# Half expert tiles through the full tiles' products, and another order of steps at the end of the state space layer

## The chip, the cores and the metric

The kernel runs on one core of a Trainium2 chip. The metric is the device time of one execution in microseconds (us), lower is better. The time before is 1714.96 us, the median of three runs (1714.86 to 1715.92).

## What is computed

The input u is 2 x 2048 tokens of 256 features. Four layers follow each other, each with a layernorm ahead of it and a residual sum behind it:

```
x = u
x = x + state_space(layernorm(x))   # projection to z, x, B, C, dt; causal convolution of 4 taps and silu;
                                    # scan h = h*exp(dt*A) + dt*x*B, y = h.C + D*x; y*silu(z), RMS norm, projection
x = x + experts(layernorm(x))       # 8 experts, every token goes to its best 2
x = x + attention(layernorm(x))     # 16 heads, over the batch dimension (2 entries)
x = x + experts(layernorm(x))       # the same weights again

experts(x):
    scores = x @ Wr.T + br                       # softmax; the two best by scores + biases, weights made to sum to 1
    y[n] = (silu(x @ Wl1[n][:, :512] + bl1a) * (x @ Wl1[n][:, 512:] + bl1b)) @ Wl2[n] + bl2
    out = sum over a token's two experts of weight * y[n]
```

All data are float32. An expert's matrices have 256 x 1024 (1 MB) and 512 x 256 (0.5 MB) elements.

## The kernel before

**Experts.** Class `Experts` computes an expert layer as a list of tiles: 256 token slots (two halves of 128) of one expert each. A routing step (`prepare`) ranks the experts for a group of 512 tokens (there are eight groups, `order`), counts by two products with 128 x 32 outputs (`pk`, L363 and L364) how many tokens each expert has so far, and so gives each token its slot. `enter` then writes the tokens' numbers and weights into a table in DRAM, by eight indirect transfers a group, issued by POOL (L433); it is a generator that gives control back after each of them, in the second layer after every other one.

A tile is started when its slots are full. `plan_early` chooses full tiles while groups still come in ("early" tiles, named `fe` in the first layer and `ge` in the second); `plan` chooses the rest from the final counts (`f` and `g`). In the first layer 21 early tiles (fe0 to fe20) are planned behind groups 3 to 7, in the second 9. What an expert has beyond whole tiles of 256 may fit a half tile of 128 slots: `plan` makes five half tiles per layer (`NIN`), and two more that run only if a count says so (`tc.If(beyond > 0)`).

Per tile: `rows` loads the tile's part of the table (SP, L656), `load` the expert's matrices and biases (SP, L668 to L674), `gather` the tokens (POOL, L683). `turn` transposes them on TensorE (`pxs`, L709; copy `xT`, L713). `up` computes the two products with Wl1 and gates them: for a full tile four parts, `up_part`, of four products each, with the weights' 128 columns standing in the array and 256 tokens moving (L722), then silu on ACT (`sa`, L730) and bias and product on DVE (`gT`, L731). `down` computes the product with Wl2 (`pf`, L792), adds bias and weight (L804, L805), and adds the rows to the residual in DRAM by indirect transfers (L816).

A half tile takes another way in `up` and `fold`: the tokens stand and 512 columns of Wl1 move (L750), ACT and DVE copy the two results `u` of 128 x 512 to SBUF, and eight transposes (`put`, L773) turn them back; then come four silu steps (L778) and four gating steps (L779) of 128 x 128. The transposes are issued in `fold`, behind the `down` of the tile before.

**Order of the work.** SP runs in the written order throughout; inside `run` POOL, ACT and DVE do too. Elsewhere the framework's scheduler orders PE, ACT, DVE and POOL. The state space layer steps through 32 chunks of 128 tokens (`chunk_front`, `chunk_back`, `chunk_out`). Three lists of generators are stepped between its parts: `aside` (projection and routing of other groups), `late` (`entering`: the table transfers, and behind them `plan_early`; each is also placed on POOL behind the chunk's POOL instruction just before) and `tiles` (`ffn.early`: the early tiles, which use PSUM bank B alone, with two buffers). Behind the last chunk the kernel finishes `aside`, then `late`, then plans, then finishes the early tiles; then `run` works through the other tiles with three tiles of lookahead. The attention layer does the same with `last`, whose early tiles go between attention's steps; it calls `last.plan()` behind all of them.

Lines: routing L300 to L410, `enter` L412 to L450, `plan_early` L452 to L513, `plan` from L515, tiles L648 to L894, state space layer L899 to L1242, attention L1256 to L1508.

Of the kernel before, what the change touches and what calls it, by code (L numbers as in the profile page):

```python
# [46 lines left out]
def kernel(  # L47
# [35 lines left out]
    def bank(tag, name):  # L83
        return ps.tile([P, 512], F32, tag=tag, name=name)
# [195 lines left out]
    class Experts:  # L280
# [454 lines left out]
        def up(self, i, between=None):  # L735
            t = self.ts[i]
            nm = t["nm"]
            pool = fe if i % 2 else self.f2
            t["gT"] = pool.tile([P, NHT, TT], F32, tag="gT", name=f"gT_{nm}", bufs=1)
            if t["nh"] == 2:  # L740
                for j in range(NHT):
                    self.up_part(t, j, "AB"[j % 2])
                    if between is not None and j == 1:
                        between()
                return

            for q in range(2):
                p = bank("AB"[q], f"pab_{nm}_{q}")
                for k in range(KD):
                    nc.tensor.matmul(  # L750
                        p,
                        t["xT"][:, k, :],
                        t["w1"][:, k, q * FH : (q + 1) * FH],
                        start=(k == 0),
                        stop=(k == KD - 1),
                    )
                u = self.f2.tile([P, FH], F32, tag=f"u{q}", name=f"u{q}_{nm}", bufs=1)
                if q:
                    nc.vector.tensor_copy(u, p)
                else:  # L760
                    nc.scalar.copy(u, p)
                t["u", q] = u

        def fold(self, i):
            t = self.ts[i]
            nm = t["nm"]
            if t["nh"] == 2:
                return
            ps2 = []
            for q in range(2):  # L770
                p = bank("AB"[q], f"put_{nm}_{q}")
                for j in range(NHT):
                    nc.tensor.transpose(p[:, j * P : (j + 1) * P], t["u", q][:, j * P : (j + 1) * P], ident)  # L773
                ps2.append(p)
            sa = self.f2.tile([P, FH], F32, tag="sh", name=f"sh_{nm}", bufs=1)
            for j in range(NHT):
                c = slice(j * P, (j + 1) * P)
                nc.scalar.activation(sa[:, c], ps2[0][:, c], AF.Silu, bias=t["b1"][:, j : j + 1])  # L778
                nc.vector.scalar_tensor_tensor(  # L779
                    t["gT"][:, j, :P], ps2[1][:, c], t["b1"][:, NHT + j : NHT + j + 1], sa[:, c], ALU.add, ALU.mult  # L780
                )

        def down(self, i, tag, then):
            t = self.ts.pop(i)
# [67 lines left out]
        def run(self):  # L852
# [3 lines left out]
            with (  # L856
# [8 lines left out]
                for i in range(first, n - 1):  # L865
                    self.fetch(i + ahead + 2, i + ahead + 1, gather=False)
                    if i == first + 6:
                        with tc.manual_schedule(engines={mybir.EngineType.PE}):
                            beyond = nc.values_load(self.beyond[0:1, 0:1], min_val=0, max_val=NHF - NIN)
                            self.up(i)  # L870
                    else:
                        self.up(i)
                    self.turn(i + 1)
                    if i > first:
                        self.down(i - 1, "C", i + ahead)
                    else:
                        for h in range(2):
                            self.gather(i + ahead, h)
                    self.fold(i)
                    if i == first + 2:  # L880
                        yield
                self.up(n - 1, lambda: self.down(n - 2, "C", None))
                self.down(n - 1, "C", None)
                with tc.If(beyond > 0):
                    for tile in self.more:
                        i = len(self.seq)
                        self.seq.append(tile)
                        self.fetch(i + 1, i + 1)
                        self.turn(i)
                        self.up(i)  # L890
                        self.fold(i)
                        self.down(i, "C", None)

    ffn = Experts("f", tc.dram_tile([NT + TT, DM], F32, name="resid"))  # L894
# [3 lines left out]
    with tc.tile_pool(name="ssm1", bufs=1) as s1, tc.tile_pool(name="ssm2", bufs=2) as s2:  # L898
# [306 lines left out]

        def entering(n, group):
            if n < len(order):
                for _ in range(4 if n < 4 else 9):
                    yield
            yield from ffn.enter(*group)  # L1210
            if n in EARLY:
                ffn.plan_early(n, EARLY[n], group[2])
# [25 lines left out]
            done = (b, s, t, y)  # L1238
        chunk_out(*done)
        aside.add(routing(*done[:2]))  # L1240
        aside.rest()
        late.rest()  # L1242
    ssm_w.__exit__(None, None, None)

    attw = ctx.enter_context(tc.tile_pool(name="attw", bufs=1))
    w_qkv_sb = attw.tile([P, KD, 3, AW], F32, name="w_qkv_sb")
    w_o_sb = attw.tile([P, NA, DM], F32, name="w_o_sb")
    ffn.plan()
    tiles.rest()
    late = ffn.run()  # L1250
    next(late)
# [8 lines left out]
    with tc.tile_pool(name="att1", bufs=1) as a1, tc.tile_pool(name="att2", bufs=2) as a2:  # L1260
# [36 lines left out]
        def entered():  # L1297
            while routed:
                n, group = routed.pop(0)
                yield from last.enter(*group)  # L1300
                if n in EARLY:
                    last.plan_early(n, EARLY[n], group[2])
                    tiles.step()
# [200 lines left out]
        while aside.waiting:  # L1504
            aside.step()
            tiles.step()
        last.plan()
        tiles.rest()  # L1508

    for _ in last.run():  # L1510
# [62 lines left out]
```

## Time and profile before

| | |
|---|---|
| median of three runs | 1714.96 us |
| the profiled execution | 1728.29 us |
| its span, first to last instruction | 1726.6 us |
| mean granted TensorE clock | 0.97 |
| busy: PE / DVE / POOL / ACT | 1595.6 / 900.0 / 734.6 / 673.9 us |
| DMA | 231.27 MB, mean 134 GB/s |
| chain that ended last: PE / DVE / DMA / POOL | 66% / 11% / 10% / 5% |
| half tiles' products `pab_f`, `pab_g` (L750) | 40 + 40 instructions of 128 x 512, mean 592 ns |
| their transposes `put_f`, `put_g` (L773) | 40 + 40 of 128 x 128, mean 273 ns |
| table transfers `table_f` from 655 to 690 us | 15, median 958 ns on POOL |

All profile rows come from one profiled execution, which is slower than the median. Times in a timeline count from the span's start. "PE" is matrix products on TensorE (transposes too), "PEld" the loads of the standing operand, "SPq" SP's queue of transfers. The length of a product's row includes the time until its last result is out, so products that follow each other overlap in the timeline; the chain of waits shows them end to end. A name stands for all buffers of that name: `pab_fe` is the first layer's early tiles, `pab_f` the others.

### The profile page before, as it was taken

Reading aid. Unit: us, or ns where it says so; the run is one execution under the profiler, and the core shown is the slowest. Engines: PE = TensorE matmul, PEld = TensorE weight load, DVE = VectorE, ACT = ScalarE, POOL = GpSimd, SP = SyncE. Lnnn points to the kernel's source line nnn. Section 1 sums busy time; section 2 is a strip of 40 time slices with the busy share of each in tenths; the row PEclk is TensorE's granted clock in tenths of the full one; section 3 lists DMA queues with packets and bytes.
Section 4 is the critical chain, followed back from the end, with each engine's and each line's share of the span. In section 5 each row is a group of like instructions: output and inputs, shape, how many; then the busy total and the mean of one; then the engine's idle time right before and its main releaser. Section 6 shows DMA issues by size and latency. Waiting matters only on the chain.

```text
span 1726.6 us, 21824 instructions
## 1 busy us (share of the span) xinstructions
PE 1595.6 (92%) x6928; PEld 1182.0 (68%) x6928; DVE 900.0 (52%) x2481; ACT 673.9 (39%) x1348; POOL 734.6 (43%) x702
## 2 busy tenths in 40 slices
PE   6997888989989996999998999899999799999997
PEld 4565555766767775788884475465768678888886
DVE  6877888838557465222237648457454522222222
ACT  4886877856556542223332102001120222333322
POOL 3346456446446565444442003403241643545443
PEclk9998998999989998999999999999999999999998
DMA  4121211734435353789842413606453668888882
GB/s 154 50 73 27 86 62 32 229 99 144 112 70 173 86 169 84 205 246 322 229 112 77 85 39 63 86 14 135 141 117 103 143 185 242 227 223 224 229 213 45
DMA packets 174742, 231.27 MB, mean 134 GB/s; under 512 B 45920, under 2 KB 138080, under 8 KB 174368
## 3 DMA queue, kind: packets, MB, share of 16 engines
q1 hardware_dynamic: 143520, 193.42, 37.7%
q0 software_dynamic: 31104, 36.42, 11.8%
q8 instruction: 56, 0.92, 0.2%
q14 instruction: 62, 0.51, 0.1%
HBM read 192.72 MB, written 37.06 MB: 133 GB/s over the span
## 4 chain that ended last, share of the span: by engine, by line
PE 66%; DVE 11%; DMA 10%; POOL 5%; issue 3%; ACT 3%; SPq 1%; DVEq 0%; POOLq 0%; ACTq 0%
PE pab_g L722 8%; PE pao L1462 6%; PE pq L1368 5%; PE pab_fe L722 5%; PE pab_f L722 4%; PE pf_g L792 4%; PE pab_ge L722 3%; PE pvd L1442 3%; PE pf_fe L792 3%; DVE xc L1047 3%; PE pk L1368 3%; PE pf_f L792 2%; PE pi L1143 2%; DMA lb<-sums 2%; DMA out_dram<-y_g,tab_g 2%
## 5 line engine op out<-in xcount | busy, mean ns | idle before, releaser
L722 PE MATMUL pab_fe<-xT_fe,w_fe 128*128 128x256 f32 x672 | 160.8, 395 | 26.9 <-DVE gT_fe L731 19.7
L722 PEld LDWEIGHTS pab_fe<-xT_fe,w_fe 128*128 128x128 f32 x672 | 130.7, 198 | 55.2 <-DVE gT_fe L731 24.3
L722 PE MATMUL pab_g<-xT_g,w_g 128*128 128x256 f32 x736 | 162.9, 379 | 0.0
L722 PEld LDWEIGHTS pab_g<-xT_g,w_g 128*128 128x128 f32 x736 | 139.4, 190 | 19.1 <-ACT xT_g L713 0.4
L816 POOL DMA_INDIRECT out_dram<-y_g,tab_g x51 | 80.3, 1574 | 141.4 <-DVE y_g L805 67.1
L1368 PE MATMUL pq<-w_qkv_sb,axT 128*128 128x512 f32 x256 | 117.9, 600 | 0.4 <-DVE qk L1387 0.4
L1047 DVE SCALAR_TENSOR_TENSOR xc<-pre,conv_w_sb,xc 128x512 f32<-128x512 f32 x144 | 112.4, 790 | 5.9 <-ACT xc L1039 5.2
L1462 PE MATMUL pao<-w_o_sb,o 128*128 128x256 f32 x512 | 112.4, 380 | 1.2 <-DVE o L1450 1.2
L1462 PEld LDWEIGHTS pao<-w_o_sb,o 128*128 128x128 f32 x512 | 96.9, 190 | 17.5 <-DVE o L1450 2.4
L731 DVE SCALAR_TENSOR_TENSOR gT_g<-pab_g,b_g,sa_g 128x256 f32<-128x256 f32 x92 | 44.5, 484 | 117.5 <-ACT sa_g L730 103.9
L730 ACT ACTIVATE sa_g<-pab_g,b_g 128x256 f32<-128x256 f32 x92 | 43.5, 473 | 154.4 <-PE pab_g L722 135.8
L433 POOL DMA_INDIRECT table_g<-pay_g,at_g x64 | 62.4, 975 | 88.0 <-DVE w_g L409 55.0
L1030 PE MATMUL pc<-xT,w_in_sb 128*128 128x512 f32 x192 | 94.8, 623 | 0.4 <-ACT xc L1039 0.4
L792 PE MATMUL pf_g<-w_g,gT_g 128*128 128x256 f32 x408 | 92.9, 379 | 0.0
L1084 ACT ACTIVATE lt<-lb,cum 128x128 f32<-128x128 f32 x256 | 82.8, 393 | 22.1 <-DMA lb<-sums 22.1
L1368 PEld LDWEIGHTS pq<-w_qkv_sb,axT 128*128 128x128 f32 x256 | 48.7, 193 | 59.5 <-issue 56.7
L731 DVE SCALAR_TENSOR_TENSOR gT_fe<-pab_fe,b_fe,sa_fe 128x256 f32<-128x256 f32 x84 | 39.6, 480 | 94.3 <-ACT sa_fe L730 88.9
L722 PE MATMUL pab_ge<-xT_ge,w_ge 128*128 128x256 f32 x288 | 70.0, 401 | 16.1 <-DVE gT_ge L731 10.6
L816 POOL DMA_INDIRECT resid<-y_fe,tab_fe x42 | 67.2, 1600 | 35.6 <-DVE y_fe L805 14.4
L792 PE MATMUL pf_fe<-w_fe,gT_fe 128*128 128x256 f32 x336 | 80.5, 393 | 1.4 <-DVE gT_fe L731 1.2
L792 PEld LDWEIGHTS pf_g<-w_g,gT_g 128*128 128x128 f32 x408 | 75.4, 190 | 9.3 <-DVE gT_g L731 0.2
L1383 ACT ACTIVATE kd<-pk 128x512 f32<-128x512 f32 x32 | 19.1, 597 | 159.2 <-PE pk L1368 88.6
(493 smaller groups left out, 3456.6 us busy)
## 6 DMA issues: line engine op xcount, KB each, us to landing
w_g<-in_wl_dram SPq DMA_DIRECT2D x28, 1024.0 KB
w_fe<-in_wl_dram SPq DMA_DIRECT2D x21, 1024.0 KB
lb<-sums SPq DMA_DIRECT2D x32, 512.0 KB
w_f<-in_wl_dram SPq DMA_DIRECT2D x16, 1024.0 KB
o<-prob SPq DMA_DIRECT2D x32, 512.0 KB
w_g<-in_wl_dram SPq DMA_DIRECT2D x28, 512.0 KB
w_fe<-in_wl_dram SPq DMA_DIRECT2D x21, 512.0 KB
w_ge<-in_wl_dram SPq DMA_DIRECT2D x9, 1024.0 KB
```

Of the source, the lines that this page charges most:

```text
L433: i = nc.gpsimd.indirect_dma_start(out=self.table, out_offset=bass.IndirectOffsetOnAxis(ap=at[:, t, c : c + 1], axis=0), in_=pay[:, t, c, ...
L722: nc.tensor.matmul(p[:, q * n : (q + 1) * n], t["w1"][:, k, c * P : (c + 1) * P], t["xT"][:, k, :], start=(k == 0), stop=(k == KD - 1),)
L730: nc.scalar.activation(sa[:, :n], p[:, 0:n], AF.Silu, bias=t["b1"][:, i : i + 1])
L731: nc.vector.scalar_tensor_tensor(t["gT"][:, i, :n], p[:, n : 2 * n], t["b1"][:, NHT + i : NHT + i + 1], sa[:, :n], ALU.add, ALU.mult)
L792: nc.tensor.matmul(pos[h][:, h * DM : (h + 1) * DM], t["gT"][:, j, h * P : (h + 1) * P], t["w2"][:, j, :], start=(j == 0), stop=(j == NHT ...
L816: j = nc.gpsimd.indirect_dma_start(out=self.acc if self.direct else self.acc[: self.seq[i][4] or NT + TT, :], out_offset=bass.IndirectOffs ...
L1030: nc.tensor.matmul(pc, w_in_sb[:, k, DI + c * P : DI + (c + 1) * P], xT[:, k, :], start=(k == 0), stop=(k == KD - 1),)
L1047: nc.vector.scalar_tensor_tensor(xc[:, c, :], pre[:, c, j : j + TG], conv_w_sb[:, c, j : j + 1], xc[:, c, :], ALU.mult, ALU.add,)
L1084: nc.scalar.activation(lt[:, i, :], lb[:, i, :], AF.Relu, bias=g["cum"][:, t, i : i + 1], scale=-1.0)
L1368: nc.tensor.matmul(p, src[:, k, t * P : (t + 1) * P], w_qkv_sb[:, k, j, half * TG : (half + 1) * TG], start=(k == 0), stop=(k == KD - 1),)
L1442: nc.tensor.matmul(pvd, w_qkv_sb[:, k, 2, c * P : (c + 1) * P], xd[:, k, :], start=(k == 0), stop=(k == KD - 1),)
L1462: nc.tensor.matmul(po[:, j * DM : (j + 1) * DM], o[i][:, c, (t + j) * P : (t + j + 1) * P], w_o_sb[:, c, :], start=(c == 0), stop=(c == NA ...
```

## The change

1. `up` sends half tiles through `up_part` too, with `n = 128`: the weights stand and 128 tokens move, 16 products, with silu and gate part by part. `fold` goes, and the copies `u`, with it.
2. Behind the state space layer's last chunk, each step of `aside` and each step of `late` is followed by a step of `tiles`. `ffn.plan()` is called there as soon as all 21 early tiles are planned, ahead of the last group's table transfers, instead of behind them. `entering` waits four steps instead of nine before the transfers of group 7.
3. In the attention layer `last.plan()` is called ahead of the last group's transfers, inside `entered`, instead of behind everything.

```diff
@@ -737,48 +737,10 @@
             nm = t["nm"]
             pool = fe if i % 2 else self.f2
             t["gT"] = pool.tile([P, NHT, TT], F32, tag="gT", name=f"gT_{nm}", bufs=1)
-            if t["nh"] == 2:
-                for j in range(NHT):
-                    self.up_part(t, j, "AB"[j % 2])
-                    if between is not None and j == 1:
-                        between()
-                return
-
-            for q in range(2):
-                p = bank("AB"[q], f"pab_{nm}_{q}")
-                for k in range(KD):
-                    nc.tensor.matmul(
-                        p,
-                        t["xT"][:, k, :],
-                        t["w1"][:, k, q * FH : (q + 1) * FH],
-                        start=(k == 0),
-                        stop=(k == KD - 1),
-                    )
-                u = self.f2.tile([P, FH], F32, tag=f"u{q}", name=f"u{q}_{nm}", bufs=1)
-                if q:
-                    nc.vector.tensor_copy(u, p)
-                else:
-                    nc.scalar.copy(u, p)
-                t["u", q] = u
-
-        def fold(self, i):
-            t = self.ts[i]
-            nm = t["nm"]
-            if t["nh"] == 2:
-                return
-            ps2 = []
-            for q in range(2):
-                p = bank("AB"[q], f"put_{nm}_{q}")
-                for j in range(NHT):
-                    nc.tensor.transpose(p[:, j * P : (j + 1) * P], t["u", q][:, j * P : (j + 1) * P], ident)
-                ps2.append(p)
-            sa = self.f2.tile([P, FH], F32, tag="sh", name=f"sh_{nm}", bufs=1)
             for j in range(NHT):
-                c = slice(j * P, (j + 1) * P)
-                nc.scalar.activation(sa[:, c], ps2[0][:, c], AF.Silu, bias=t["b1"][:, j : j + 1])
-                nc.vector.scalar_tensor_tensor(
-                    t["gT"][:, j, :P], ps2[1][:, c], t["b1"][:, NHT + j : NHT + j + 1], sa[:, c], ALU.add, ALU.mult
-                )
+                self.up_part(t, j, "AB"[j % 2])
+                if between is not None and j == 1:
+                    between()
 
         def down(self, i, tag, then):
             t = self.ts.pop(i)
@@ -876,7 +838,6 @@
                     else:
                         for h in range(2):
                             self.gather(i + ahead, h)
-                    self.fold(i)
                     if i == first + 2:
                         yield
                 self.up(n - 1, lambda: self.down(n - 2, "C", None))
@@ -888,7 +849,6 @@
                         self.fetch(i + 1, i + 1)
                         self.turn(i)
                         self.up(i)
-                        self.fold(i)
                         self.down(i, "C", None)
 
     ffn = Experts("f", tc.dram_tile([NT + TT, DM], F32, name="resid"))
@@ -1205,7 +1165,7 @@
 
         def entering(n, group):
             if n < len(order):
-                for _ in range(4 if n < 4 else 9):
+                for _ in range(9 if 3 < n < len(order) - 1 else 4):
                     yield
             yield from ffn.enter(*group)
             if n in EARLY:
@@ -1238,14 +1198,21 @@
             done = (b, s, t, y)
         chunk_out(*done)
         aside.add(routing(*done[:2]))
-        aside.rest()
-        late.rest()
+        while aside.waiting:
+            aside.step()
+            tiles.step()
+        planned = False
+        while late.waiting:
+            if not planned and len(ffn.seq) == EARLY[len(order) - 1]:
+                ffn.plan()
+                planned = True
+            late.step()
+            tiles.step()
     ssm_w.__exit__(None, None, None)
 
     attw = ctx.enter_context(tc.tile_pool(name="attw", bufs=1))
     w_qkv_sb = attw.tile([P, KD, 3, AW], F32, name="w_qkv_sb")
     w_o_sb = attw.tile([P, NA, DM], F32, name="w_o_sb")
-    ffn.plan()
     tiles.rest()
     late = ffn.run()
     next(late)
@@ -1297,6 +1264,8 @@
         def entered():
             while routed:
                 n, group = routed.pop(0)
+                if n == len(order):
+                    last.plan()
                 yield from last.enter(*group)
                 if n in EARLY:
                     last.plan_early(n, EARLY[n], group[2])
@@ -1504,7 +1473,6 @@
         while aside.waiting:
             aside.step()
             tiles.step()
-        last.plan()
         tiles.rest()
 
     for _ in last.run():
```

## The prediction

> **What bounds the kernel now.** I read the page first: PE is busy for 92% of the span and carries 66% of the chain that ended last, so a change is worth what it takes off PE's own work, or off the places where PE stands still. The page's 40 slices (43 us each) show where that is: counted from 0, slices 16 to 20 and 32 to 38 stand at 9 for PE, slice 15 (648 to 691 us) at 6, and the group list has no idle time before `pab_g`. So the two `run` stages are bound by PE's work, and the end of the state space layer by something else.
>
> Next the chain of waits around the first half tile (763 to 792 us), for the work that the first edit replaces:
>
> ```profile
> 767.82 2.59 PE pf_f L792 x12
> 770.41 3.43 PE pab_f L750 x8
> 773.84 0.44 PE pxs_f L709 x4
> 774.28 3.46 PE pf_f L792 x16
> 777.73 0.87 PE put_f L773 x8
> 778.61 6.91 PE pab_f L722 x32
> ```
>
> Columns are start, length, engine, what. Each row begins where the last ended: the 512-column products (3.43 us) and the transposes back (0.87 us) lie wholly on the path, 4.30 us per half tile. The same pair stands in the second layer (PE's timeline: L750 at 1475.52, L773 at 1482.85).
>
> Then PE's timeline at the end of the state space layer:
>
> ```profile
> 661.19 2.05 PE L1172 MATMUL po<-w_out_sb,yt 128*128 128x264 f32 x8 [0.73 <-ACT yt L1169]
> 670.30 0.64 PE L363 MATMUL pk_f<-sel_f,tri 128*128 128x32 f32 x2 [7.06 <-DVE sel_f L357]
> ...
> 672.95 9.00 PE L722 MATMUL pab_fe<-xT_fe,w_fe 128*128 128x256 f32 x32 [0.68 <-issue]
> 682.12 4.05 PE L792 MATMUL pf_fe<-w_fe,gT_fe 128*128 128x256 f32 x16 [0.17 <-issue]
> 686.00 0.60 PE L709 MATMUL pxs_fe<-ident,xs_fe 128*128 128x128 f32 x4
> 690.66 8.66 PE L722 MATMUL pab_fe<-xT_fe,w_fe 128*128 128x256 f32 x32 [4.05 <-issue]
> ...
> 716.98 7.17 PE L722 MATMUL pab_fe<-xT_fe,w_fe 128*128 128x256 f32 x32 [0.68 <-ACT xT_fe L713]
> ```
>
> In brackets is the idle time and who ended it. PE stands 7.06 us while DVE routes the last group, because the next early tile (fe15) is queued behind that group's two counting products. Afterwards the same 32 products take 9.00 and 8.66 us instead of 7.17: by the stage table the granted clock is 0.66 from 663.2 to 672.9, then 0.86 and 0.89, and 1.00 from 702.7. Last, the queues of SP and POOL there:
>
> ```profile
> 667.35 0.38 SPq L318 DMA_DIRECT2D xnd_f<-xn_f  x1
> 676.08 0.39 SPq L656 DMA_DIRECT2D tab_fe<-table_f  x1
> 677.30 0.39 SPq L668 DMA_DIRECT2D w_fe<-in_wl_dram  x1
> ```
>
> ```profile
> 664.81 1.05 POOL L244 TENSOR_TENSOR rs_f<-rs_f,mhalf 128x4 f32<-128x4 f32 x1 [2.58 <-DVE rs_f L243]
> 666.05 1.18 POOL L433 DMA_INDIRECT table_f<-pay_f,at_f  x1 [0.20 <-issue]
> 672.78 0.95 POOL L433 DMA_INDIRECT table_f<-pay_f,at_f  x1 [0.30 <-issue]
> 678.66 0.98 POOL L683 DMA_INDIRECT xs_fe<-xnd_f,tab_fe  x1 [4.92 <-PE pab_fe L722]
> ```
>
> Six of group 7's table transfers stand behind the layernorm's power; the next tile's row table waits for them, and the weights of tile fe16 wait behind it on SP.
>
> **Half tiles.** Ten half tiles run (five in each layer; L750 has 40+40 instructions, eight per tile; the two behind the branch don't run). Each code-level product is two instructions. Removed: 8 of 512 columns, 3.43 us, and 8 transposes, 0.87 us. Added: 32 instructions of 128 columns, each with its own weight load. The nearest row is `pb` L1103, a product of 128 columns: the chain has it as "0.22 PE pb L1103 x2" (629.71 us), 0.11 each, and `pi` L1143 with only 64 columns takes "1.73 ... x16" (635.54), 0.108 each. So 64 and 128 columns cost the same; the load hides behind 128 columns. 32 x 0.111 = 3.55 us, against 4.30: −0.75 us, ten times −7.5.
>
> The Trainium skill speaks against this. "TensorE: Matmul & The Clock Gate", section "Back-to-back issue gap", gives a sustained 81 ns per product of 128 columns beside its weight load, and 131 ns for 512: per column 2.5 times as dear. By that ratio the half tile would cost an estimated 3.43 x 2.47 = 8.5 us instead of 4.30, +42 us over ten. Here a row of the very shape exists, so I take 0.11; the rule stays as a rival. Bounds: at the transposes' 0.109 the gain is 8; at 0.134 each it is nil.
>
> Around it: DVE loses a 128x512 copy, ACT as well, and both keep four 128x128 steps (340 to 377 ns on each). A part now takes PE 0.89 us; ACT and DVE need 0.37 and 0.34 us for it, in parallel queues over four banks, so PE is not held. The next tile's transposed input comes behind four short ACT steps (1.5 us) instead of one copy, with 3.46 us of `pf` covering it. SP and POOL issue the same DMAs in the same order here. DMA share is 0.70 to 0.91 through most of both stages, so a stage shorter by 4 us in some 165 (2%) still fits; one stretch (790 to 810 us, share 1.08, PE busy 18.44 of 20) may swallow a tile's 0.75. I take −7, range −8 to 0.
>
> **Alternating steps at the end of the state space layer.** In the built order of each engine, fe15's input transposes now stand before the last-but-one `po`, half of its first part before the last one, and the counting products only in fe16's middle. Sum on PE from 656.70 (second-last `pty`) to 752.53 (first `pab_f`), 95.8 us. Work in it: two `pty` at 0.44 and two `po` at 1.78, six tiles of 0.44 + 6.91 + 3.46 = 10.81, `pk` 0.45, three more pairs of transposes 0.66: 70.4. So 25.4 us are idle, cold clock and waits. What stays: 0.68 for each of five input copies (3.4), 1.1 for the gathers of f0 and f1. What is new: bank B has two buffers, and DVE must finish part j before PE starts part j+2. DVE's queue now has the four `xn` (1.43 us, behind POOL's power) between parts 0 and 1 of fe15, and ACT reloads its table twice (1.28 each) before part 3: about 0.9 + 0.5 us. In fe16 the counting products take a bank, and some 30 short planner steps (0.1 each) stand between its parts: 0.65 + 0.3. With 0.3 of `po` delay: 2.6. So 25.4 − 4.5 − 2.6 = −18.3 us.
>
> Who else was moved. SP: fe16's weights (two issues, two biases) now stand ahead of the `xnd` store and the row tables, so they go at some 665 instead of 677.3; fe16 needs them at about 675. Before, DMA moved them between 677 and 684 (up to 386 GB/s, then almost nothing). Row tables of fe17 and fe18 follow at about 670, since one table transfer instead of six stands behind the power. POOL: five more of group 7's eight transfers (1.3 us each with the gap) now go between earlier steps, into POOL's idle gaps there: 0.9 us before 622.1, 1.0 before 640.5, 3.3 before 654.3 (two of them), 1.0 before 656.6. At most 0.4 us each is left over, ahead of `ss` or `resid`, which wait for other work anyway; without the gaps it would be 1.3 each, 6.5 in all. Behind the power POOL has one table transfer, `resid` of fe15 (two of 1.9 with the gap, ready at 675, when fe15's `pf` and `y` are done), then the gathers of fe17 and fe18, issued from 679, then group 8's eight transfers (10 us), then `resid` of fe16 and the gathers of fe19 (698, needed at 709). fe17's second gather (680) is needed at 686. A gather here lands 4.8 us (736.79) to 6.7 us (614.89) after its start: on time, or 1 us late. This is the tightest spot. Unknown is the 4.05 us before 690.66: its own row names no one, fe16's weights had landed, and no cause shows. I take it as gone with the cold stretch; if it comes again, with its cold 1.6 us, the gain drops to 12.6, with a late gather 11.5. Range −21 to −11.
>
> The shorter wait of group 7's entries (4 steps instead of 9) is what moves those transfers; priced above.
>
> **The attention layer's planner.** `last.plan()` moves up in the code, but in the built order PE, DVE, POOL and SP have the same sequence and waits there as before, but for half tiles. Zero.
>
> **Sum.** −18.3 − 7 = −25.3. The profiled execution took 1728.3 us (span 1726.6), so about 1703 there; it stands 13.3 above the median of the unprofiled runs, whose work is the same. On the median: 1714.96 − 25.3 = 1690.
>
> **Rivals.**
> 1. Alternation stops short: fe15 starts early, but fe17 waits for its gather behind POOL's queue, or the unexplained stall comes again. For it: POOL already serializes there. Against: seven transfers left the queue. Then −11.5 − 5 = 1698. Chance 0.25.
> 2. Half tiles bring nothing: 32 loads with their semaphores reach 0.134 us each. Against: `pb`. −18.3 alone: 1697. Chance 0.1.
> 3. Slower: the weight load is exposed in a long stream of 128-column products, as the skill's figure says; place: all ten half tiles; price +42, net +24, 1739. It decides from 0.19 us per instruction on, where 32 of them cost 6.13 us and the ten eat the 18.3. Against: 64 columns already run at 0.108 to 0.112 in streams of 16. Chance 0.05.
> 4. The moved steps do nothing, because the last group's routing still holds PE: then −7, 1708. The built order speaks against it. Chance 0.03.
> The main case, 1690, has 0.57 (1684 to 1695).
>
> Less than 0.2% (3.4 us) is what a measurement of this kernel can't tell from no change. Faster: all but rival 3 and a little for unseen waits, 0.92; same 0.02; slower 0.06. The range takes in rivals 1 and 2 and the bounds (−29 plus 2 for spread, −11): 1684 to 1704.
>
> **What would show it.** `pab_f` with 128 columns: 32 in 3.5 to 3.7 us without idle before `pf`, and no `put`. PE's idle before `pk_f` near zero, granted clock 1.00 from 660 to 700, weights of fe16 issued near 665, first `pab_f` near 734 instead of 752.5. Wrong, if 32 instructions take over 4.3 us, if `pxs_fe` of fe17 waits for a gather by over 2 us, or if time is given back between 734 and the first attention product.

## The result and the profile after

The changed kernel takes 1697.34 us (median of 6 runs, 1692.32 to 1706.89) where the kernel before, run beside it, takes 1715.44 (6 runs, 1713.57 to 1720.16): a ratio of 0.9894, with a 95% interval of 0.9869 to 0.9919, so 18.1 us less (13.9 to 22.5). The forecast was 1690 and a range of 1684 to 1704: the sign and the range hold, the gain was put 7 us too large, and 1697.34 lies outside the 1684 to 1695 of its main case. The profiled execution of the changed kernel lasted 1695.92 us, its span 1694.1. In this kernel's file the lines have moved: `pf` is L754, the copy-out of `y` L767, `po` L1132, `pty` L1128.

First the work that the half tiles do now: the chain of waits of the changed kernel around its first half tile (start, length, engine, what).

```profile
755.97 2.59 PE pf_f L754 x12
758.56 3.57 PE pab_f L722 x32
762.13 0.44 PE pxs_f L709 x4
762.56 3.46 PE pf_f L754 x16
766.02 6.91 PE pab_f L722 x32
```

One row of 32 products, 3.57 us, stands where the kernel before has 3.43 and 0.87: 0.73 us less, and the next product follows without a gap. Each instruction costs 0.1116 us with its own weight load (3.57 by 32).

Then PE's timeline of the changed kernel at the end of the state space layer (start, length, engine, line, operation, in brackets the idle time in front and who ended it).

```profile
664.18 1.03 PE L722 MATMUL pab_fe<-xT_fe,w_fe 128*128 128x256 f32 x4
665.07 2.05 PE L1132 MATMUL po<-w_out_sb,yt 128*128 128x264 f32 x8
...
671.75 1.99 PE L722 MATMUL pab_fe<-xT_fe,w_fe 128*128 128x256 f32 x8 [0.31 <-DVE gT_fe L731]
676.16 2.43 PE L754 MATMUL pf_fe<-w_fe,gT_fe 128*128 128x256 f32 x10 [0.88 <-DVE gT_fe L731]
683.26 0.30 PE L363 MATMUL pk_f<-sel_f,tri 128*128 128x32 f32 x2
684.63 3.72 PE L722 MATMUL pab_fe<-xT_fe,w_fe 128*128 128x256 f32 x16 [0.85 <-DVE gT_fe L731]
693.04 7.17 PE L722 MATMUL pab_fe<-xT_fe,w_fe 128*128 128x256 f32 x32 [0.68 <-ACT xT_fe L713]
729.81 0.61 PE L709 MATMUL pxs_f<-ident,xs_f 128*128 128x128 f32 x2 [1.62 <-DMA xs_f<-xnd_f,tab_f]
740.68 4.70 PE L722 MATMUL pab_f<-xT_f,w_f 128*128 128x256 f32 x21
```

The next early tile's first part stands ahead of the last `po`, and the counting products (`pk_f`) have no idle time in front where they had 7.06 us. The waits in its place are short: 0.31, 0.88, 0.85. Full rounds take 7.17 us, since the granted clock no longer falls: the table by stages gives 1.00 in each stretch of 12 us from 656 to 740. The queues of SP and POOL in the same place:

```profile
668.98 0.39 SPq L668 DMA_DIRECT2D w_fe<-in_wl_dram  x1
676.42 1.55 SPq L656 DMA_DIRECT2D tab_fe<-table_f  x2
678.82 0.38 SPq L668 DMA_DIRECT2D w_fe<-in_wl_dram  x1
```

```profile
669.94 1.18 POOL L433 DMA_INDIRECT table_f<-pay_f,at_f  x1 [0.20 <-issue]
683.14 1.00 POOL L683 DMA_INDIRECT xs_fe<-xnd_f,tab_fe  x1 [0.30 <-issue]
688.23 1.00 POOL L433 DMA_INDIRECT table_f<-pay_f,at_f  x1 [0.30 <-DVE cump_f L548]
```

One table transfer is left behind the layernorm's power, the weights of tile fe16 go 8.3 us earlier than before, and the next weights (678.82) wait for nothing of the last group. The last group's eight transfers start at 688.23 and still stand in a row on POOL: the built order puts nothing between them, whatever steps the code puts there.

### The profile page after: what moved, and what is told of

It reads as the page before. It is cut to its first block, busy times and chain, and to the rows that moved or that the text cites. A ratio compares the mean times of both kernels' runs of the same rounds, so it can differ in the third digit from the quotient of the medians.

```text
span 1694.1 us, 22151 instructions
## 1 busy us (share of the span) xinstructions
PE 1584.1 (94%) x7088; PEld 1193.8 (70%) x7088; DVE 897.0 (53%) x2471; ACT 670.9 (40%) x1338; POOL 736.2 (43%) x702
## 4 chain that ended last, share of the span: by engine, by line
PE 66%; DVE 12%; DMA 11%; POOL 5%; ACT 3%; issue 3%; SPq 1%; DVEq 0%; POOLq 0%; ACTq 0%
PE pab_g L722 9%; PE pao L1431 7%; PE pab_fe L722 5%; PE pq L1337 5%; PE pab_f L722 5%; PE pf_g L754 4%; PE pf_fe L754 4%; PE pab_ge L722 3%; DVE xc L1007 3%; PE pk L1337 3%; PE pvd L1411 3%; PE pi L1103 2%; DMA lb<-sums 2%; PE pc L990 2%; PE pf_f L754 2%
## 5 line engine op out<-in xcount | busy, mean ns | idle before, releaser
L722 PE MATMUL pab_g<-xT_g,w_g 128*128 128x256 f32 (+1 forms) x896 | 181.6, 361 | 0.0
L722 PEld LDWEIGHTS pab_g<-xT_g,w_g 128*128 128x128 f32 x896 | 158.5, 191 | 19.4 <-ACT xT_g L713 0.4
L730 ACT ACTIVATE sa_g<-pab_g,b_g 128x256 f32<-128x256 f32 (+1 forms) x112 | 50.9, 454 | 191.3 <-PE pab_g L722 191.3
L731 DVE SCALAR_TENSOR_TENSOR gT_g<-pab_g,b_g,sa_g 128x256 f32<-128x256 f32 (+1 forms) x112 | 51.5, 460 | 129.0 <-ACT sa_g L730 129.0
L722 PE MATMUL pab_f<-xT_f,w_f 128*128 128x256 f32 (+1 forms) x512 | 96.6, 347 | 0.0
L754 PE MATMUL pf_g<-w_g,gT_g 128*128 128x256 f32 x408 | 92.9, 380 | 0.0
L722 PEld LDWEIGHTS pab_f<-xT_f,w_f 128*128 128x128 f32 x512 | 85.5, 191 | 9.4
L754 PE MATMUL pf_fe<-w_fe,gT_fe 128*128 128x256 f32 x336 | 80.3, 392 | 2.2 <-DVE gT_fe L731 2.2
```

What stands on the lines that cost most here:

```text
L722: nc.tensor.matmul(p[:, q * n : (q + 1) * n], t["w1"][:, k, c * P : (c + 1) * P], t["xT"][:, k, :], start=(k == 0), stop=(k == KD - 1),)
L730: nc.scalar.activation(sa[:, :n], p[:, 0:n], AF.Silu, bias=t["b1"][:, i : i + 1])
L731: nc.vector.scalar_tensor_tensor(t["gT"][:, i, :n], p[:, n : 2 * n], t["b1"][:, NHT + i : NHT + i + 1], sa[:, :n], ALU.add, ALU.mult)
L754: nc.tensor.matmul(pos[h][:, h * DM : (h + 1) * DM], t["gT"][:, j, h * P : (h + 1) * P], t["w2"][:, j, :], start=(j == 0), stop=(j == NHT ...
```

## Where the time went, stage by stage

The same product ahead of the change's first instruction (a `pi` near 590 us) starts up to 8.6 us apart in the 14 profiles (587.56 to 596.19), so whole spans compare badly. Each row of this table follows one execution through four stretches, each between the starts of two named products, and gives how much longer (+) or shorter it took there than the first profile of the kernel before. Stretches: end of the state space layer (last `pi` at 653.08 to the first `pab_f` at 752.53), full tiles of the first layer (to the last tiles' `pf_f` at 895.75), end of attention (`pt_g` at 1339.75 to the first `pab_g` at 1436.00), full tiles of the second layer (to `pf_g` at 1701.19). What lies between the stretches is left out; the main part of the attention layer, some 425 us, varies there by 7 us from one execution to the next (422.6 to 429.6), on average the same with the old half tiles and with the new (425.6 and 425.8).

| execution | end of ssm | tiles f | end of attention | tiles g |
|---|---|---|---|---|
| before_third | +0.24 | +2.14 | −12.85 | 0.00 |
| half_again | −0.26 | −0.08 | −12.92 | −3.69 |
| alt_again | −13.63 | +1.06 | −12.73 | 0.00 |
| the changed kernel, first profile | −15.73 | −1.06 | −12.81 | −3.69 |
| after_third | −15.84 | −1.83 | −7.97 | −3.69 |
| late_weights | −16.01 | −1.75 | −13.01 | −3.69 |
| spread | −12.12 | −1.58 | −12.88 | −3.69 |
| double | −8.66 | −2.14 | −12.40 | −3.69 |
| later | −14.89 | −3.94 | −12.92 | −4.02 |
| before_again | +0.52 | −0.18 | −3.34 | 0.00 |
| half_only | −0.45 | −0.35 | −1.96 | −3.69 |
| alt_only | −3.88 | +1.46 | −6.57 | 0.00 |
| after_again | −4.43 | −0.21 | −1.84 | −3.69 |

The last four rows are from a second chip, on which every kernel took longer (the kernel before 1729.49 us). In later an edit moves the last `pt_g` itself back by 5.6 us, so that row counts from the eight `pt_g` ahead of it (1321.00 in the first profile), which keep their place; counted from the last `pt_g` it would read −18.42, a gain that isn't there. A stretch has to start at a product that the edit leaves where it was.

The third column is a trap. The first profiles of the two kernels differ by 32.5 us of span, and 12.81 of that lie at the end of attention; but the kernel before has the same 12.85 in another execution. The first profile of the kernel before stood still there (5.95 us of PE before 1377.50), and it takes no change of the kernel to be rid of that.

## The experiments

My theory was that of the forecast: the alternation takes the wait for the last group's routing off PE and nothing else comes in its place, and the half tiles add their 0.75 us each. The rivals: one of the two brings nothing, or a stall at the end of the state space layer comes again.

**before_again.** The kernel before, unchanged.

> The kernel before once more, for a second profile. The first profile of it took 1728.3 us where its unprofiled runs have a median of 1715.4, and holds a hole of 8.0 us in DVE's queue at 1369 us (the second layer's planner) that the changed kernel's profile does not have. If that hole belongs to one execution and not to the kernel, this profile lacks it and its span is near 1714 us, 12 below the first. If the change had removed it, it stands here again and the span is near 1726.

Measured: 1725.2 us, span 1723.5. This came from the second chip, where the kernel before has a median of 1729.49, so the span can't decide between the two. The trace says more: PE stood still again in front of fe16's first product, 3.77 us, and for 5.13 us at the end of attention, so neither stall belonged to that one execution alone; VectorE's hole there was 5.24 us and not 8.0.

**half_only and half_again.** The kernel before with the first part of the diff alone, the half tiles:

```diff
-            if t["nh"] == 2:
-                for j in range(NHT):
...
-            for q in range(2):
-                p = bank("AB"[q], f"pab_{nm}_{q}")
...
+            for j in range(NHT):
+                self.up_part(t, j, "AB"[j % 2])
```

> The kernel before with the half tiles' edit alone. Theory A (the edit is worth its work on PE wherever PE is busy): 10 x 0.73 = 7.3 us faster, 1708. Theory B (in the first layer a late gather sets the pace, so what the half tiles free becomes wait; the second layer alone gains, 5 x 0.73): 3.7 to 4.5 us faster, 1711. Rival (32 products of 128 columns are no cheaper): 1715.

> The kernel before with the half tiles alone once more; the first time it came to 0.9992 of the kernel before, where the forecast's step says -7 us (0.9959). Theory H: each half tile saves 0.73 us of TensorE, five in the second layer reach the end (-3.7 us), and of the five in the first layer most are lost to a gather that waits longer while the attention weights load: 0.9978, -3.7 to -4.5 us. Rival 1 (all ten reach the end): 0.9957. Rival 2 (none do): 1.000.

Measured: 0.9992 (0.9976 to 1.0007) and 1.0001 (0.9979 to 1.0024). The timing shows no gain, and rules out the forecast's −7 us (0.9959) for this edit alone. The traces are sharper: in the second layer the stretch is 3.69 us shorter in each execution with half tiles, and unchanged in each without, five times 0.74. In the first layer, executions without half tiles give +2.14, +1.06, −0.18, +1.46 (0 for the first profile; mean +0.9), those of half tiles without other edits there −0.08, −1.06, −1.83, −0.35, −0.21 (mean −0.7): about 1.6 of the 3.7 arrive (1.9 with spread and double counted in; by the scatter of the rows I estimate that either can be off by some 1 us). So theory H holds in the traces, −3.7 and about −1.6. The time of these kernels, which scatters by 12 to 20 us from run to run, shows less: −1.4 and +0.2 us. The sum of the traces, −5.3 us (0.9969), lies below both intervals, and where the difference stays is not shown.

**alt_only and alt_again.** The kernel before with the rest of the diff alone: the shorter wait of group 7, the alternating loops, both planners moved.

```diff
-                for _ in range(4 if n < 4 else 9):
+                for _ in range(9 if 3 < n < len(order) - 1 else 4):
...
-        late.rest()
+        while late.waiting:
...
+            late.step()
+            tiles.step()
```

> The changed kernel with the old half tiles, so the new order of steps at the end of the state space layer alone. From the two profiles the first product of the tiles behind it comes 12 us earlier than before, though the stretch ahead of it, whose order hardly changed, was 3.9 us later: the step itself 16 us. Theory A: 12 to 16 us faster, 1699 to 1703, and together with half_only the whole of the change. Rival (later stages give part of it back, since the gathers and weights of the next stage do not come earlier): less than 10 us faster, 1706 or more, with a longer wait for a gather near 790 us.

> The kernel before with the alternation and the earlier planners alone once more; the first time it came to 0.9965, with a stall of 8 to 9 us between 690 and 725. Theory A (where no such stall occurs, the alternation keeps what it gains): without a stall 12 to 14 us less than the kernel before, 0.992 to 0.993; in an execution with the stall 4 to 6 us less. Rival (the stall belongs to the alternated order): the stall is there again and the ratio at 0.9965.

Measured: 0.9965 (0.9951 to 0.9980), and 0.9924 (0.9900 to 0.9948). The second came as theory A said, with 13.63 us less at the end of the state space layer. Those are 2.1 us fewer than in the changed kernel, because PE waited 1.90 us for the first full tile's gather (1.62 there), and the next 32 products ran on a colder clock (8.77 us in place of 7.08). In the first, most of the gain went into a stall: PE waited 7.98 us before 703.64, and the next 32 products took 9.92 us in place of 7.17. The end of attention is the same with and without the moved planner (−12.73 and −12.85): zero, as forecast.

**after_again.** The changed kernel on the second chip.

> The changed kernel once more: the interval of the whole change on the same chip as its parts. Theory A: the sum of half_only and alt_only, 17 to 20 us faster, 1696 to 1698. If the parts hinder each other, less than their sum by over 3 us. In its profile 32 products of 128 columns take 3.57 us on PE's chain and the wait for a gather near 792 us (2.6 us in the first profile) stands again.

Measured: 0.9949 (0.9932 to 0.9965), 8.8 us less, where 17 to 20 were expected. The two parts alone make −1.4 and −6.1 us on this chip, −7.4 together, so they don't hinder each other. The stall is there too; PE's timeline and then ScalarE's:

```profile
690.62 0.66 PE L709 MATMUL pxs_fe<-ident,xs_fe 128*128 128x128 f32 x4 [1.63 <-issue]
699.22 9.25 PE L722 MATMUL pab_fe<-xT_fe,w_fe 128*128 128x256 f32 x32 [7.94 <-ACT xT_fe L713]
```

```profile
698.58 0.59 ACT L713 COPY xT_fe<-pxs_fe 128x512 f32<-128x512 f32 x1 [12.65 <-remote]
```

PE's transposes are over at 691.28 by the records, but ScalarE copies their result only at 698.58, and VectorE stands for 6.38 us too. The clock falls in the idle time: the next 32 products take 9.25 us in place of 7.17, at a granted clock of 0.77. Meanwhile POOL issues the eight table transfers in a row (685.31 to 695.18). That gave theory S: the eight transfers hold up the engines.

**after_third, spread, double, late_weights.** Run on one chip, beside each other.

> The changed kernel once more, for comparison with the three runs beside it. Twice its alternation stood in the trace as forecast up to 703 us (8 to 14 us ahead of the kernel before), but in one execution a stall of 8 to 9 us between 690 and 703 gave most of it back, while the last group's eight table transfers ran in a row. Theory S (the eight transfers in a row hold up the engines' completions or instructions): the stall comes again in most executions, so about 0.993 to 0.996 of the kernel before. Rival (the stall is an accident of one chip): the ratio is again near 0.989, as on the first.

> The changed kernel with the last group's eight table transfers of both layers held apart: each waits for the last product of the half of an early tile in front of it, so that on GpSimd's queue they stand one, one, two, two, one, one between gathers and adds. Theory S (the stall comes from the eight in a row): no wait over 3 us of TensorE between 685 and 735, the first product of a full tile 7 to 9 us earlier than in the run of the changed kernel beside it, and the hole of 5 to 8 us at the end of attention gone too: 10 to 16 us less than that run. Rival (the stall is instruction loading, with no tie to the transfers): it stands at its place, and the time is within 3 us of that run. A third way: the table is complete later, so the first full tile's gather waits and takes up to 5 us back ahead of 745.

```diff
+                    if final and self.paced is not None:
+                        tc.add_manual_dep(
+                            i.ins,
+                            self.paced.ins.name,
...
-            nc.vector.scalar_tensor_tensor(
+            self.paced = nc.vector.scalar_tensor_tensor(
```

> The changed kernel in which each of the last group's eight table transfers of the first layer is followed by a second one that writes the same 128 rows into a table that nobody reads: sixteen in a row, about 20 us on GpSimd in place of 10. Theory S: the stall of TensorE near 690 to 703 grows by about as long as the transfers, 16 us in place of 8, so 8 us slower than the changed kernel beside it. Rival (no tie to the transfers): the stall keeps its length; early tiles whose gathers stand behind the queue may wait up to 3 us longer.

```diff
+                    if final:
+                        k = nc.gpsimd.indirect_dma_start(
+                            out=self.table2,
...
```

Measured: after_third 0.9903 (0.9879 to 0.9927), without a stall; spread 0.9931 (0.9907 to 0.9956); double 0.9939 (0.9919 to 0.9959). On this chip theory S falls: sixteen transfers in a row made no such stall, and eight in a row made none either. On the second chip, where the stall came, neither version was run. Spreading had nothing to win and lost some: the transfers ran from 688.91 to 721.90, the first full tile's gather made PE wait 3.22 us (1.42 in after_third), and the stretch is 3.7 us longer; the ratios alone, whose intervals overlap, couldn't tell. What the double transfers cost is another thing; PE's timeline of double:

```profile
714.59 1.18 PE L718 MATMUL pxs_fe<-ident,xs_fe 128*128 128x128 f32 x4 [4.49 <-DMA xs_fe<-xnd_f,tab_fe]
716.45 9.54 PE L731 MATMUL pab_fe<-xT_fe,w_fe 128*128 128x256 f32 x32 [0.67 <-ACT xT_fe L722]
```

The gather of a tile stands behind the sixteen on POOL's queue and comes 4.49 us late; the clock falls for the next round (9.54 in place of 7.17, 2.4 us more). Together that is 6.9 us, and the stretch is 7.2 us longer than in after_third. Eight more transfers took POOL 10 us, and 4.49 of them reached PE: so POOL's queue has an estimated 5 us to spare here, where the forecast saw its tightest spot.

The fourth kernel asks for the attention weights later.

> The changed kernel in which the attention weights (4 MB) are asked for behind the eleventh full tile of the first layer instead of behind the third. In the changed kernel a gather near 800 us arrives 2.5 us late in the burst that these weights make, and the 3.7 us that five half tiles save in the first layer don't show at its end. Theory B (the burst makes the gather late): the wait near 800 falls below 0.5 us and the first layer ends 2 us earlier against its start, 2 us less in all. Rival: the burst moves to the eleventh tile and makes a gather late there, or the attention's first product waits for its weights: 0 to 3 us more.

```diff
-                    if i == first + 2:
+                    if i == first + 10:
                         yield
```

Measured: 0.9904 (0.9886 to 0.9921), the same as after_third. First a row of PE's timeline in the changed kernel's first profile, then one in late_weights:

```profile
792.17 0.90 PE L709 MATMUL pxs_f<-ident,xs_f 128*128 128x128 f32 x3 [2.62 <-DMA xs_f<-xnd_f,tab_f]
```

```profile
863.07 0.41 PE L709 MATMUL pxs_f<-ident,xs_f 128*128 128x128 f32 x2 [2.85 <-DMA xs_f<-xnd_f,tab_f]
```

The wait near 790 is gone, so the burst of 4 MB made that gather late: theory B's cause is right. But the burst makes another gather late eight tiles on, by as much: its rival has the sum, and the wait just moves with the burst.

**before_third.** The kernel before again, on yet another chip, with half_again, alt_again and later.

> The kernel before, for a profile that can be laid beside that of the changed kernel where no engine stands still for no shown reason. The first profile of the kernel before lasted 1728.29 us where its median is 1714.96; it has a stall of 4.05 us at the end of the state space layer and a hole of 8.0 us on VectorE at the end of attention, 12 us together. Theory A (both are accidents of single executions, which any of the kernels can have): a profile near 1715 us has neither, and near 1726 us it has them. Then the alternation is worth about 12.6 us against an undisturbed execution and not the forecast 18.3. Rival (the stall belongs to the order of the work before): the profile near 1715 us still has the 4 us ahead of 690.

Measured: 1722.45 us, span 1720.8. Neither held. The stall ahead of 690 is gone, and the time isn't gained. PE's timeline and SP's queue in before_third:

```profile
694.20 7.17 PE L722 MATMUL pab_fe<-xT_fe,w_fe 128*128 128x256 f32 x32 [0.68 <-ACT xT_fe L713]
708.26 5.38 PE L722 MATMUL pab_fe<-xT_fe,w_fe 128*128 128x256 f32 x16 [2.94 <-DMA w_fe<-in_wl_dram]
```

```profile
699.63 2.73 SPq L656 DMA_DIRECT2D tab_fe<-table_f  x3
703.20 0.38 SPq L668 DMA_DIRECT2D w_fe<-in_wl_dram  x1
```

And what SP waited for there (in total, times, longest):

```profile
SPq L656 <- DMA table_f<-pay_f,at_f: 13.5, 1, 13.5
```

Since PE comes to the next tile (fe17) earlier, it waits there for weights (2.94 us), and the colder clock costs another 1.66 us (5.38 in place of 3.72). SP reads three row tables (L656) ahead of these weights, and stood 13.5 us in front of them, waiting for the last group's eight transfers, the last of which starts at 695.03 on POOL; so the weights are asked for only at 703.20. In the changed kernel fe17's weights are asked for at 678.82, ahead of those transfers. Half_again shows the same wait, 3.43 us. So this part of the old order costs its 4.6 to 5.5 us in each of five executions, wait and clock together, by the one wait or the other. In the seven profiles of the alternated order outside the second chip neither wait is there.

**later.** The changed kernel with three more edits.

> The changed kernel with three more edits. In the last early tiles of both layers the next tile's transposes stand in front of the tile's second product, so that TensorE doesn't wait 0.68 us for the copy out of PSUM: four to five tiles in each layer, -2.5 to -3 us each. The first full tile's transposes are held behind the last early tile's second product, where the changed kernel has them one tile too early and waits 1.4 to 1.6 us for their gather: -1.5 us in the first layer, about as much in the second. The attention weights are asked for in four parts of 1 MB, two full tiles apart: the 2.6 us wait near 792 shrinks, -1 to -2.5 us. Theory: 7 to 11 us less than the changed kernel, 0.984 to 0.986 of the kernel before. Rival (the transposes of the next tile then wait for their gather in front of the second product, and each part of the weights makes a gather late): no gain, 0.989 to 0.991.

```diff
-                self.turn(i)
+                if not turned:
+                    self.turn(i)
...
+                turned = self.drain and i + 1 < full
+                if turned:
+                    self.turn(i + 1)
                 self.down(i, "B", None)
...
-                self.turn(first)
+                with tc.issue_after(self.pf.ins):
+                    self.turn(first)
...
-                    if i == first + 2:
+                    if i - first in (2, 4, 6, 8):
```

Measured: 1692.54 us, 0.9871 (0.9834 to 0.9907). It is the lowest ratio of all, but its interval overlaps that of the changed kernel and lies across both theory and rival, so the times decide nothing. PE's timeline of later, one early tile:

```profile
698.24 0.60 PE L709 MATMUL pxs_fe<-ident,xs_fe 128*128 128x128 f32 x4
699.49 3.72 PE L754 MATMUL pf_fe<-w_fe,gT_fe 128*128 128x256 f32 x16 [0.65 <-DVE gT_fe L731]
703.05 7.07 PE L722 MATMUL pab_fe<-xT_fe,w_fe 128*128 128x256 f32 x32
```

The first edit failed in a telling way. The 0.68 us in front of the first product are gone, and 0.65 appear in front of the second, which now meets the last gate of VectorE sooner: a tile takes 11.72 us in place of 11.79 (704.83 less 693.04 in the changed kernel). The 1.62 us for the first full tile's gather are gone, yet the first stretch is no shorter than in the changed kernel: at 672.76 fe15's second product waits 1.74 us for the copy of fe16's input, whose transposes now stand ahead of it, and runs on a colder clock (5.41 in place of 3.67). The gain that the traces show comes behind: 2 to 3 us in the first layer's full tiles, where the weights come in four parts (the one wait left, near 815, is 1.21 us). At the end of attention nothing is gained (−12.92 against −12.81): the wait of 1.67 us for the first full tile's gather is gone, but two of 1.59 and 1.90 us appear among the early tiles.

## Why the prediction was right, and where it was too large

**Half tiles, per instruction: right.** 0.1116 us measured, 0.111 taken; the path lost 0.73 us per half tile, 0.75 taken. The rule that spoke against it (the Trainium skill, "TensorE: Matmul & The Clock Gate", section "Back-to-back issue gap": 81 ns for 128 columns, 131 for 512) doesn't carry over to this kernel's f32 products: a 512-column instruction here takes 0.43 us (3.43 by 8), so per column the short one is 1.04 times as dear and not 2.5, and its own load adds no more than these 4%.

**Half tiles, the sum: too large.** The step "ten times −7.5", taken as −7, measured 3.7 + 1.6 = 5.3. In the second layer all five arrive. In the first, the stretch that the forecast named (790 to 810 us) did swallow what it could: PE waits there for a gather that comes late in the burst of the attention weights, 2.62 us in the changed kernel where it was 1.56, so a PE that is early waits longer. The row of the kernel before, beside the one at 792.17 above:

```profile
803.37 0.55 PE L709 MATMUL pxs_f<-ident,xs_f 128*128 128x128 f32 x3 [1.56 <-DMA xs_f<-xnd_f,tab_f]
```

Summed over the first layer's full tiles, such waits are 2.6 to 3.4 us in the seven profiles with new half tiles and the weights in their old place, and 1.4 to 2.8 in the five with the old ones, on average 1.1 us more. That is half of the 2.1 us that don't arrive; the other half is not located. Late_weights shows that it is the burst which makes the gather late.

**Alternation: right in mechanism, 2.5 to 4.7 us too large.** Forecast −18.3, range −21 to −11; measured −15.73 and −15.84 in the changed kernel and −13.63 alone, where no stall came. Idle time before `pk_f` is zero, the clock 1.00, fe16's weights went at 668.98 in an execution that was 3.88 us late, so at 665.1 as forecast. The first `pab_f` came at 740.68, which without those 3.88 us is 736.8, against 734. The missing 2.6 us are not waits. From `pty` at 660.58 to the first `pab_f` the changed kernel takes 80.1 us, where the forecast came to 77.5. PE's idle time in it is 6.6 us, less than the 7.1 taken (the wait for the first full tile's gather is 1.62 where 1.1 was taken, the others are shorter in sum). What is left, 73.5 us, stands against 70.4: the term that was mis-sized is PE's own work. The forecast took a tile as 0.44 + 6.91 + 3.46 = 10.81 us, from rows of the chain in a stream without waits. With its one wait of 0.68 such a tile would take 11.49; early tiles start 11.79 us apart in the changed kernel (693.04 to 704.83), and 11.80 apart in the kernel before (716.98 to 728.78). The extra 0.3 us a tile, some 1.8 of the 3.1 us for six tiles, was never idle time that an order could take away, but the forecast counted it among its 25.4 us; the rest is spread over the other rows.

**The 4.05 us before 690.66: gone, but not for the forecast's reason.** The forecast saw no cause and took them "as gone with the cold stretch". What PE waited for does stand in the first profile of the kernel before, on ScalarE:

```profile
690.02 0.58 ACT L713 COPY xT_fe<-pxs_fe 128x512 f32<-128x512 f32 x1 [7.56 <-remote]
```

The transposes are over at 686.60 by the records, ScalarE is idle, and it copies their result 3.4 us later. Before_again and half_only show the same (3.1 and 2.8 us), and it is the picture of the stall in after_again, but shorter. Before_third has them gone in the old order, after a stretch just as cold (10.15 us for fe15's 32 products), with a wait for weights in their place. What the alternation removes for certain is the order on SP that made those weights late. The forecast had looked at fe16's weights alone, and not at those of the tile behind; that its number held is luck.

**The moved attention planner: zero**, as forecast.

**Sum.** By the traces −15.1 (mean of 15.73, 15.84, 13.63) − 1.6 − 3.7 = −20.4 where no stall comes; by the medians −18.1, with an interval of 4 us to each side. Of the 7 us that the forecast was off, 3.2 are the alternation, 1.7 the half tiles, and 2.3 lie within what the medians can tell. The range held in its upper part, which stood for rivals 1 and 2 (1698 and 1697); in the first profile neither came, so that the time falls on their price is chance. Rival 1 also counts the half tiles as 5 us, where the main case has 7 and gives no reason for the difference. On the second chip only 8.8 us were left (0.9949), because of the stall, which the forecast had as part of rival 1 and priced at 5.65 us; it measured 8 of waiting and 2 of clock.

**What stays open.** The cause of that stall, a copy on ScalarE that comes late though its transposes are over. It came in all four profiles from the second chip, in the old order (3.77 and 3.42 us) as in the alternated one (7.98 and 7.94), and in one of ten from elsewhere, the first of the kernel before. So it belongs neither to the alternated order nor to one chip alone, and why it is twice as long in the alternated order isn't shown. The transfers in a row don't suffice for it (double, and every profile without it). The loading of instructions stays possible: in after_again one load of 8 KB began at 691.16 and took 2.27 us, the next began at 699.63, as the stall ended. Against it: in after_third three such loads ran within 9 us at this place without a stall, and a load of 16 KB stands at 689.82 in the first profile of the kernel before, where the stall ends, and at 689.51 in half_again, which has none. A version that loads no instructions there wasn't tried, so this is a guess.

Open too is what each edit of the alternation brings: the shorter wait of group 7, the alternating loops and the earlier `ffn.plan()` were always run together. The traces show the new order of PE and of SP's queue that the three make, not their shares.

## What to carry to other kernels

When one engine's order is changed, follow each queue two tiles on: an order that stalls PE in one place can hide a late load in the next, and only a change that moves both gains. A wait that is hidden by putting other work in front can come back one instruction later if the next producer was only just in time (0.68 became 0.65). And compare executions stretch by stretch, with at least two profiles of the old kernel, and from a product that no edit has moved: 12.8 us of the difference between the first two profiles here had nothing to do with the change.

## What the hardware showed that I had not expected

- Products of 64 and of 128 columns in f32 cost the same, 0.108 and 0.112 us per instruction with its own weight load; cutting 512 columns into four costs almost nothing (3.57 us in place of 3.43 for the same work).
- Two executions of one kernel can differ by 12.8 us at one place (end of attention) with the same instructions in the same order.
- An idle stretch of 3 us costs more than itself: after 2.94 us of waiting the next 16 products took 1.66 us longer (granted clock 0.72), after 4.49 us the next 32 took 2.4 longer (0.75), after 7.94 us 2.1 longer (0.77). Shorter waits go either way: after 1.74 us (later) the next 16 took 1.74 longer, at 0.67, while after 1.62 us in the changed kernel the next 32 took their usual 7.08.
- Beside a burst of 4 MB on SP's queue, PE waited 1.4 to 2.9 us for a gather of 128 rows of 1 KB, at either of two places; with the burst in four parts, 1.2.
